# Moving the first expert's input and a set of matrix copies into the attention of a two-layer transformer, and adding unread products at its start

## The chip, the cores and the metric

The kernel runs on one core of a Trainium2 chip. A core has a matrix engine (TensorE, PE in the profile), a vector engine (VectorE, DVE), a scalar engine (ScalarE, ACT), GpSimd (POOL) and SyncE (SP), which here does nothing but issue DMA transfers. Each engine works through its own queue in order, and waits on semaphores for others. The metric is the time of one launch in microseconds (us). A profile also lists the clock that TensorE was granted, as a share of its full speed.

## The reference, cut to what matters

The input is 2048 tokens (4 x 512 in layer 0) of width 256. Each layer takes the normalised input and adds an attention and a mixture of experts to it:

```
x  = L0_attn_x
xn = layernorm(x)
x  = x + attention0(xn) + experts0(xn)
xn = layernorm(x)
x  = x + attention1(xn) + experts1(xn)
```

- attention0: 16 heads of width 16 over 4 key/value heads, queries and keys through low-rank products (64 and 32), rotary positions, causal softmax, output product.
- experts0: 8 experts, the best 2 for every token. Each expert takes at most 1280 rows (256 wide) and computes `(gelu(rows @ Wa) * (rows @ Wg)) @ Wout`, with 512 columns in each half; the result times the gate is added to the token's row.
- attention1: attention of every token to 32 learned patterns with sparsemax in place of softmax.
- experts1: 8 small gated experts (width 128), the best 2 for every token, and two shared ones.

## The kernel before, in words

*Start-up.* Tokens are taken in groups of 512. For each group, `fetch` loads the rows into `xg` (two buffers), in two halves; the second half of group 0 is issued by ACT, all else by SP. VectorE takes the statistics (`bn_stats`), GpSimd the inverse roots by Newton steps, VectorE normalises, TensorE turns the rows by transposes (`flip`), and the low-rank products go to `low`, a tile of 104 partitions x 2048. Before these can be used in the scores, the key tiles `ks` are filled with a pattern of zeros and ones (`clean_k` on ACT, `clean_q` on GpSimd for the query tiles).

*Attention of layer 0.* It runs twice over the keys: once for the maxima (`s<-ks,q`, VectorE reductions, then `flip_max`, whose result `mtT` goes through `mr` into the query tiles by a DMA `q<-mr`), once for the scores (`sc<-q,ks`, exponentials `es` on ACT, masks on GpSimd, products `av`). A quarter of the tokens has its output projection (`po`) when its heads are done, and the sum `xo` is stored to `x1` in DRAM. The rows that go to the experts are scattered to `buf` in DRAM by GpSimd's indirect DMAs, 258 wide: 256 values, the row's place and its gate.

The order of all this is not left to the framework: a planner in the kernel keeps a model of each engine's time (`T`, with constants such as `ISSUE = 620` ns for one DMA issue), picks the next piece of TensorE work among `candidates()`, and emits pieces for other engines from a list of `jobs`. `later(engine, duration, ready, f, then, rank)` puts a piece on that list, due from `ready` (in ns of the model's time), and `flush` emits it when the model has the engine free. Each instruction that it emits is pinned in program order by `pin`, `mm`, `flip` and `sdma`. Instructions that are not pinned are placed by the framework's scheduler.

*Experts of layer 0.* For each of 8 experts: `load_rows` brings 1152 rows of `buf` into `rows` by one DMA, `transposed` turns them with 18 transposes into `inT`, `places` copies out the rows' places (`to`) and gates, and `feed_forward` works in three chunks of 384 rows: for four column blocks, `pa` and `pg` (four instructions each), Gelu on ACT, product `hT` on VectorE; then three products `py` over `hT`, scaled to `ys` on VectorE, and added to `x1` by GpSimd's indirect DMAs. Rows of expert e+1 are loaded during expert e, weights of expert e+2 after it. (More than 1152 rows of one expert are dealt with behind a condition that is not met here.)

*Layer 1.* Its first matrices (`wqT`, `wk`, `wv` and seven smaller ones) are loaded by ACT's queue at the end of the attention and folded in the experts' stage. Its experts read their matrices with indirect DMAs from `wall`, a DRAM tile that 40 copies from DRAM to DRAM fill: five for each expert, two of them of `fg`, two of `fu`, one of `fd`. In the source they stand in the loop over layer 0's experts; the scheduler put all 40 at the head of SP's queue. Layer 1 then follows a plan of its own.

The PSUM pools of the attention are `ps2`, `pssc` and `psav`; those of the experts' stage `moetp` and `moeps`.

Of the kernel before, what the change touches and what calls it, by code (L numbers as in the profile page):

```python
# [145 lines left out]
def moe_transformer_kernel(  # L146
# [122 lines left out]
    csp = cctx.enter_context(tc.tile_pool(name="csp", bufs=1, side="right"))  # L269
    cs_sb = csp.tile([P, 2, S], F32, name="cs_sb")  # L270

    wi0 = cs_sb[:, 0].rearrange("p (c f) -> p c f", c=2)
    wt0 = cs_sb[:, 1, 0:4 * E].rearrange("p (c e) -> p c e", c=4)
    with ExitStack() as actx:
# [9 lines left out]
        psav = actx.enter_context(tc.tile_pool(name="psav", bufs=1, space=PSUM))  # L284
        low = attw.tile([96 + NE, NT], F32, name="low")
        wq16 = attw.tile([64, 2, 16, 16], F32, name="wq16")
# [28 lines left out]
        def sdma(*args):  # L315
            pin(SP.dma_start(*args))
# [52 lines left out]
        def lows(grp):  # L369

            ps = ps2.tile([P, 512], F32, tag="ps2", name="lw")
            for dc in range(2):
                mm(ps[:96 + NE], lhsT=wa_sb[:, dc], rhs=st[grp]["xnT"][:, dc], start=dc == 0, stop=dc == 1)
            pin(A.copy(low[:, 512 * grp:512 * grp + 512], ps[:96 + NE]))

# [264 lines left out]
        def load_out_weights():  # L640
# [3 lines left out]
            sdma(bout_sb, bout.broadcast_to([P, E]))  # L644

        xss = {}
        ways = bass_types.dram_disjoint_views(buf[:], 4)
# [8 lines left out]
        def dispatch(ti, k):  # L656
# [3 lines left out]
                                     xss[ti], None, bounds_check=NSLOT - 1, oob_is_err=False))  # L660

# [431 lines left out]
        def candidates():  # L1093
# [59 lines left out]
        while pos["av"] < len(avq) or jobs or projects or scat["ti"] < NTILE:  # L1153
            prefetch()
            refetches()
            keys_back()
            scatter()
            flush()
            cand = [z for z in candidates() if z[1] < INF]

            events = [job[4] for job in jobs if job[4] > T["PE"]] + [T["S"], T["V"], T["G"], T["A"]]
            events = [t for t in events if t > T["PE"]]
            best = min(cand, key=lambda z: z[:2]) if cand else None
            if best and best[1] <= min(events + [INF]) + 400:
                best[2]()
# [48 lines left out]

    sq = {}
# [3 lines left out]
    kp_sb = fold_tile(P, 2, NPAT)  # L1219
    A.dma_start(kp_sb, kpT.rearrange("(c p) m -> p c m", p=P))  # L1220
    bqk = fold_tile(P, 2, 2)
    A.dma_start(bqk, bqk2)
    bv_sb = fold_tile(1, E)
    A.dma_start(bv_sb, bv)
    A.dma_start(wo_sb, wo.rearrange("(c p) m -> p c m", p=P))
    A.dma_start(bo_sb, bo.broadcast_to([P, E]))
    A.dma_start(gw_sb, gw.rearrange("(c p) m -> p c m", p=P))
    A.dma_start(lb_sb, lb)


    with tc.tile_pool(name="moe", bufs=2) as mp, tc.tile_pool(name="moeh", bufs=3) as hp, \
            tc.tile_pool(name="moetp", bufs=2, space=PSUM) as mtp, \
            tc.tile_pool(name="moeps", bufs=2, space=PSUM) as mps:
        tiles = CAP0 // P

        def load_rows(e):
            rows = mp.tile([P, tiles, ROW], F32, tag="rows", name="rows")
            SP.dma_start(rows, buf[CAP * e:CAP * e + CAP0].rearrange("(c p) d -> p c d", p=P))
            return rows
# [20 lines left out]
        def feed_forward(wi, wt, inT, n, to, gates_e, c0, x1s):  # L1260
# [22 lines left out]
        last = bass_types.dram_disjoint_views(x1[:], 3)  # L1283
        rows = load_rows(0)
        for e in range(NE):
            wi, wt = experts[e]
            to, gates_e = places(rows, tiles)
            inT = mp.tile([P, 2, CAP0], F32, tag="inT", name="inT")
            transposed(rows, tiles, inT)
            if e + 1 < NE:  # L1290
                rows = load_rows(e + 1)
            for c in range(2):
                SP.dma_start(wall[P * e:P * e + P, P * c:P * c + P], fg[:, c, e])
# [760 lines left out]
```

## Time and profile before

| what | value |
|---|---|
| median of 3 runs | 2124.32 us (2123.4 to 2124.34) |
| the profiled execution's own time | 2125.51 us |
| its span, from the first to the last instruction | 2123.8 us |
| mean granted clock of TensorE | 0.952 |
| start-up, to the first score tile | 0 to 63.0 us |
| attention of layer 0, to the last `po` | 63.0 to 1201.0 us |
| seam: to the first expert's transposes | 1201.0 to 1209.3 us |
| experts of layer 0 | 1209.3 to 1605 us |
| layer 1 | 1605 to 2124 us |

How to read the profile's rows. A row of the timeline has the start in us, the duration in us (of a group of several instructions, from the first to the last), the engine (`SPq` and `ACTq` are DMA issues by that engine, `PEld` a weight load), the source line, the operation, output and inputs by the program's names, shape and type, and the count. In brackets stands the idle time before the instruction, and whose work ended it. A row of the table by stretch has the stretch, its length, the busy time and count of instructions for PE, PEld, DVE, ACT and POOL, the granted clock, the DMA engines' busy share and the GB/s moved. On the page, `PEclk` has one digit for each of 40 equal slices of the span, in tenths of full speed (9 is 0.9 and more).

### The profile page before, as it was taken

How to read it: one execution, taken by the hardware profiler on the slowest of the kernel's cores; microseconds unless marked ns; L12 is line 12 of the kernel's file. 1: busy time of each engine (PE TensorE's matmuls, PEld its weight loads, DVE VectorE, ACT ScalarE, POOL GpSimd, SP SyncE). 2: the span in 40 equal slices, each digit the busy share in tenths (PEclk: the TensorE clock that was granted, in tenths of full speed). 3: DMA queues.
4: the chain of work that ended last, by engine and by line, in shares of the span. 5: the costliest groups of instructions: out<-in, count | busy, mean ns of one | idle time of the engine just before them, and what ended most of it. 6: DMA issues, size and time to landing. Idle time of an engine off the chain costs nothing. (4 is left out here: it accounts for less than half of the span.)

```text
span 2123.8 us, 26286 instructions
## 1 busy us (share of the span) xinstructions
PE 1927.7 (91%) x9525; PEld 1070.7 (50%) x9534; DVE 1386.4 (65%) x1943; ACT 913.7 (43%) x1834; POOL 721.2 (34%) x914
## 2 busy tenths in 40 slices
PE   4689999899999999999999799999998998878886
PEld 2344443444444444444443366666765755666664
DVE  4576688676787578778784122222226599999896
ACT  3044456355555655665567411111112333554452
POOL 5232211443444333431101022222230088466551
PEclk8599899899999999999999899999999799999999
DMA  5433321242132322321200333333223022444417
GB/s 148 127 118 103 101 71 38 82 130 67 59 101 84 100 91 64 92 85 32 91 11 11 123 82 75 77 77 77 52 28 105 11 80 88 134 146 145 154 59 238
DMA packets 141384, 188.98 MB, mean 89 GB/s; under 512 B 15678, under 2 KB 109252, under 8 KB 141251
## 3 DMA queue, kind: packets, MB, share of 16 engines
q1 hardware_dynamic: 114672, 135.03, 21.1%
q0 software_dynamic: 23552, 50.46, 9.4%
q10 hardware_dynamic: 3026, 1.77, 0.3%
q8 instruction: 77, 1.26, 0.2%
q14 instruction: 57, 0.46, 0.1%
HBM read 100.74 MB, written 90.66 MB: 90 GB/s over the span
## 5 line engine op out<-in xcount | busy, mean ns | idle before, releaser
L510 ACT ACTIVATE es<-sc 128x512 f32<-128x512 f32 (+3 forms) x1280 | 599.6, 536 | 457.7 <-PE sc L310 447.0
L471 DVE TENSOR_REDUCE part<-s 128x2 f32<-128x1024 f32 (+3 forms) x640 | 650.4, 1059 | 210.5 <-PE s L310 209.3
L310 PE MATMUL sc<-q,ks 128*128 128x512 f32 (+3 forms) x1280 | 425.5, 418 | 19.5 <-ACT es L510 18.9
L310 PEld LDWEIGHTS sc<-q,ks 128*128 128x128 f32 x1280 | 211.7, 191 | 249.0 <-ACT es L510 174.5
L310 PE MATMUL av<-es,va 128*32 128x512 f32 (+3 forms) x2560 | 303.2, 552 | 3.4 <-POOL es L512 1.8
L512 POOL TENSOR_SCALAR_AFFINE_SELECT es<-es 128x256 f32<-128x256 f32 x256 | 103.4, 407 | 561.5 <-ACT es L510 560.5
L310 PE MATMUL s<-ks,q 64*128 64x512 f32 (+3 forms) x1280 | 253.1, 447 | 33.8 <-DVE part L471 11.2
L138 DVE TENSOR_TENSOR srt<-srt 128x1024 f32<-128x1024 f32 (+3 forms) x224 | 224.0, 1036 | 7.6 <-ACT to L138 0.5
L310 PEld LDWEIGHTS s<-ks,q 64*128 64x128 f32 x1280 | 111.6, 189 | 200.6 <-DVE part L471 110.5
L1279 POOL DMA_INDIRECT x<-ys,to x72 | 111.5, 1549 | 294.6 <-DVE ys L1277 165.5
L1270 DVE TENSOR_TENSOR hT<-ge,pg 128x384 f32<-128x384 f32 x96 | 53.2, 554 | 178.1 <-PE pg L1267 176.9
L1269 ACT ACTIVATE ge<-pa 128x384 f32<-128x384 f32 x96 | 47.1, 490 | 269.4 <-PE pa L1267 269.4
L138 POOL DMA_INDIRECT oe<-xn,to x80 | 109.3, 1367 | 76.0 <-ACT xn L138 56.2
L1267 PE MATMUL pa<-inT,wi 128*128 128x384 f32 x336 | 123.3, 486 | 0.0
L1267 PE MATMUL pg<-inT,wi 128*128 128x384 f32 x336 | 122.1, 486 | 0.0
L138 POOL DMA_INDIRECT buf<-xn,slot x64 | 87.7, 1371 | 99.9 <-DVE rc L138 80.7
L1274 PE MATMUL py<-wt,hT 128*128 128x256 f32 x504 | 112.2, 379 | 0.0
L138 ACT COPY srt<-srt 128x1024 f32<-128x1024 f32 (+2 forms) x80 | 67.2, 840 | 101.6 <-DVE srt L138 89.4
L310 PEld LDWEIGHTS av<-es,va 128*32 128x32 f32 x2560 | 55.7, 109 | 100.5 <-issue 76.3
L1274 PEld LDWEIGHTS py<-wt,hT 128*128 128x128 f32 x504 | 95.8, 190 | 17.5
L1277 DVE TENSOR_SCALAR ys<-py,gates 128x256 f32<-128x256 f32 x72 | 34.8, 484 | 86.0 <-PE py L1274 86.0
L1267 PEld LDWEIGHTS pg<-inT,wi 128*128 128x128 f32 x336 | 63.3, 190 | 42.7
(265 smaller groups left out, 2308.2 us busy)
## 6 DMA issues: line engine op xcount, KB each, us to landing
q<-qd SPq DMA_DIRECT2D x64, 256.0 KB
buf<-zero SPq DMA_DIRECT2D x20, 516.0 KB
buf<-zero SPq DMA_DIRECT2D x20, 514.0 KB
xn<-buf SPq DMA_DIRECT2D x20, 514.0 KB
rows<-buf SPq DMA_DIRECT2D x8, 1161.0 KB
qd<-hi SPq DMA_DIRECT2D x16, 512.0 KB
qd<-lo SPq DMA_DIRECT2D x16, 512.0 KB
xn<-oe SPq DMA_DIRECT2D x16, 512.0 KB
```

The costliest lines, as they stand in the source:

```text
L138: return lambda *a, **k: self.tc.keep_in_program_order(f(*a, **k))
L310: pin(PE.matmul(*args, **kw))
L471: pin(V.tensor_reduce(parts[j][:, i, 2 * pair:2 * pair + 2, kb], sc[:, :, :n], AX.X, ALU.max))
L510: pin(A.activation(es[:, g % 2, :n], sc[:, :n], AF.Exp, scale=0.25))
L512: pin(G.affine_select(es[:, :, 0:P], es[:, :, 0:P], pattern=[[0, 2], [1, P]], compare_op=ALU.is_ge, fill=0.0, base=0, channel_multiplier=-1))
L1267: PE.matmul(ps[:, :n], lhsT=wi[:, dc, col:col + P], rhs=inT[:, dc], start=dc == 0, stop=dc == 1)
L1269: A.activation(ge[:, :n], pa[:, :n], AF.Gelu)
L1270: V.tensor_tensor(hT[:, f, :n], ge[:, :n], pg[:, :n], ALU.mult)
L1274: PE.matmul(py, lhsT=hT[:, f, P * i:P * i + P], rhs=wt[:, f], start=f == 0, stop=f == 3)
L1277: V.tensor_scalar(ys, py, gates_e[:, c:c + 1], None, ALU.mult)
L1279: G.indirect_dma_start(x1s[c % len(x1s)], bass.IndirectOffsetOnAxis(ap=to[:, c:c + 1], axis=0), ys, None, compute_op=ALU.add)
```

## The change

It has six parts.

1. The 40 copies into `wall` are now pinned in the attention by `copy_matrices`, in eight sets of five, due from 320 us of the model's time on, one set every 60 us.
2. `clean_k(0)` is no longer emitted ahead of everything: all five fills are jobs due from 2, 7, 12, 17 and 22 us. In the new order ACT issues the second half of group 0's load first.
3. Unread products: in model time in which TensorE has nothing to do, before the first `av`, a bf16 product of the tile of ones (128x256) is emitted for every 160 ns, into a `psav` tile that nobody reads. There are 98: 48 at the head of TensorE's queue, 2 and then 48 after the third group's transposes and low-rank products, before the first score tile.
4. The first expert's rows: three SP loads of 384 rows (`load_rows0`) after the last scatter, and 18 transposes with three VectorE copies (`turn_rows0`) after the last maxima. They lie in `low`, which now has all 128 partitions and outlives the attention, and in `cs_sb`. The experts' stage starts with these, so `load_rows(0)` and `transposed` for expert 0 go.
5. Ten loads for layer 1 go from ACT's queue to SP's, in the loop at e = 1 (`load_fold`).
6. `py` has a PSUM pool of its own, and the two buffers of `rows` are a part of `low` and one tile.

On TensorE the seam now has this order: the last `av`, one `po`, two `pa` of the first expert, seven `po`, then `pg` and `pa` of the first expert in turn.

```diff
-        low = attw.tile([96 + NE, NT], F32, name="low")
+    low = csp.tile([P, NT], F32, name="low")
+    rows0 = low[:, 0:CAP0 // P * ROW].rearrange("p (c d) -> p c d", d=ROW)
+    inT0 = [low[:, CAP0 // P * ROW + 768 * i:CAP0 // P * ROW + 768 * i + 768] for i in range(2)] + [cs_sb[:, 1, 4 * E:4 * E + 768]]
...
+        def copy_matrices(e):
+            for c in range(2):
+                sdma(wall[P * e:P * e + P, P * c:P * c + P], fg[:, c, e])
+                sdma(wall[P * e:P * e + P, E + P * c:E + P * c + P], fu[:, c, e])
+            sdma(wall[P * e:P * e + P, 2 * E:3 * E], fd[:, e])
...
+        def load_rows0(i):
+            sdma(rows0[:, 3 * i:3 * i + 3], buf[384 * i:384 * i + 384].rearrange("(c p) d -> p c d", p=P))
+        def turn_rows0(i):
+            tp = ps2.tile([P, 2, 512], F32, tag="ps2", name="tp0")
+            for dc in range(2):
+                for c in range(3):
+                    flip(tp[:, dc, P * c:P * c + P], rows0[:, 3 * i + c, P * dc:P * dc + P], ident)
+            pin(V.tensor_copy(inT0[i], tp[:, :, 0:384]))
...
+            if pos["u"] == len(units) and at.get("turned", 0) < 3:
+                i = at.get("turned", 0)
+                t = max(now, when("row0", i), free2[-2])
+                def turn():
+                    at["turned"] = i + 1
+                    t = use2(1500, "t", 0, lambda: turn_rows0(i))
+                    free2.append(on("V", 1000, t))
+                yield t - now + 200, t, turn
...
-        clean_k(0)
...
-        for i in range(1, NKS):
-            later("A", 2560, 6000 + 4000 * i, lambda i=i: clean_k(i), None, 2)
+        for i in range(NKS):
+            later("A", 2560, 2000 + 5000 * i, lambda i=i: clean_k(i), None, 2)
...
+        for e in range(NE):
+            later("S", 5 * ISSUE, 320000 + 60000 * e, lambda e=e: copy_matrices(e), None, 2)
...
+        idle = ones.bitcast(BF16)
+        def product():
+            if "idle" not in st[0]:
+                st[0]["idle"] = psav.tile([P, 512], F32, tag="av", name="idle")
+            mm(st[0]["idle"][:, 0:256], lhsT=idle[:, 0:P], rhs=idle, start=True, stop=True)
...
+                if pos["av"] == 0:
+                    idle_for += t1 - T["PE"]
+                    while idle_for > 160:
+                        idle_for -= 160
+                        if (not free2[-1] and idles < 48) or (when("low", 1) < INF and not pos["u"]):
+                            idles += 1
+                            product()
                 T["PE"] = t1
...
+            if at.get("w0") and scat["ti"] == NTILE and not at.get("r0"):
+                at["r0"] = 1
+                for i in range(3):
+                    later("S", ISSUE, T["PE"] + 8000, lambda i=i: load_rows0(i),
+                          lambda t, i=i: at.update({("row0", i): t}), 2)
...
-    for nm, ap in (("wqT", wqT), ("wk", wk), ("wv", wv)):
-        sq[nm] = fold_tile(P, 2, E)
-        A.dma_start(sq[nm], ap.rearrange("(c p) m -> p c m", p=P))
...
+    def load_fold():
+        for v, ap in ((sq["wqT"], wqT), (sq["wk"], wk), (sq["wv"], wv), (kp_sb, kpT), (wo_sb, wo), (gw_sb, gw)):
+            SP.dma_start(v, ap.rearrange("(c p) m -> p c m", p=P))
+        SP.dma_start(bqk, bqk2)
...
+            tc.tile_pool(name="moepy", bufs=2, space=PSUM) as mpy, \
...
+        rows_of = [rows0, mp.tile([P, tiles, ROW], F32, tag="rows", bufs=1, name="rows")]
         def load_rows(e):
-            rows = mp.tile([P, tiles, ROW], F32, tag="rows", name="rows")
+            rows = rows_of[e % 2]
...
-                py = mps.tile([P, E], F32, tag="py", name="py")
+                py = mpy.tile([P, E], F32, tag="py", name="py")
...
-        rows = load_rows(0)
+        rows = rows0
         for e in range(NE):
             wi, wt = experts[e]
             to, gates_e = places(rows, tiles)
-            inT = mp.tile([P, 2, CAP0], F32, tag="inT", name="inT")
-            transposed(rows, tiles, inT)
+            if e == 0:
+                parts_in = inT0
+            else:
+                inT = mp.tile([P, 2, CAP0], F32, tag="inT", name="inT")
+                transposed(rows, tiles, inT)
+                parts_in = [inT[:, :, s0:s0 + STEP] for s0 in range(0, CAP0, STEP)]
             if e + 1 < NE:
                 rows = load_rows(e + 1)
-            for c in range(2):
-                SP.dma_start(wall[P * e:P * e + P, P * c:P * c + P], fg[:, c, e])
-                SP.dma_start(wall[P * e:P * e + P, E + P * c:E + P * c + P], fu[:, c, e])
-            SP.dma_start(wall[P * e:P * e + P, 2 * E:3 * E], fd[:, e])
+            if e == 1:
+                load_fold()
             for s0 in range(0, CAP0, STEP):
-                feed_forward(wi, wt, inT[:, :, s0:s0 + STEP], STEP, to, gates_e, s0 // P, last if e == NE - 1 else [x1[:]])
+                feed_forward(wi, wt, parts_in[s0 // STEP], STEP, to, gates_e, s0 // P, last if e == NE - 1 else [x1[:]])
```

More of the change, by code (lines that the diff above doesn't have):

```diff
@@ L270, in moe_transformer_kernel @@
     cs_sb = csp.tile([P, 2, S], F32, name="cs_sb")
+    low = csp.tile([P, NT], F32, name="low")
+    rows0 = low[:, 0:CAP0 // P * ROW].rearrange("p (c d) -> p c d", d=ROW)
+    inT0 = [low[:, CAP0 // P * ROW + 768 * i:CAP0 // P * ROW + 768 * i + 768] for i in range(2)] + [cs_sb[:, 1, 4 * E:4 * E + 768]]
+    inT0 = [v.rearrange("p (c n) -> p c n", c=2) for v in inT0]
     wi0 = cs_sb[:, 0].rearrange("p (c f) -> p c f", c=2)
@@ L373, in lows @@
                 mm(ps[:96 + NE], lhsT=wa_sb[:, dc], rhs=st[grp]["xnT"][:, dc], start=dc == 0, stop=dc == 1)
-            pin(A.copy(low[:, 512 * grp:512 * grp + 512], ps[:96 + NE]))
+            pin(A.copy(low[:96 + NE, 512 * grp:512 * grp + 512], ps[:96 + NE]))
         def logits(grp):
@@ L1152, in moe_transformer_kernel @@
             later("S", ISSUE, 340000 + 40000 * i, lambda i=i: clear(buf1, i), None, 2)
-        while pos["av"] < len(avq) or jobs or projects or scat["ti"] < NTILE:
+        idle = ones.bitcast(BF16)
[3 more added lines that the diff above has]
+            mm(st[0]["idle"][:, 0:256], lhsT=idle[:, 0:P], rhs=idle, start=True, stop=True)
+        idle_for, idles = 0, 0
+        while pos["av"] < len(avq) or jobs or projects or scat["ti"] < NTILE or at.get("turned", 0) < 3:
             prefetch()
@@ L1213, in fold_tile @@
         return v
-    sq = {}
-    for nm, ap in (("wqT", wqT), ("wk", wk), ("wv", wv)):
-        sq[nm] = fold_tile(P, 2, E)
-        A.dma_start(sq[nm], ap.rearrange("(c p) m -> p c m", p=P))
[L1219 to L1228, printed above, removed]
+    sq = {nm: fold_tile(P, 2, E) for nm in ("wqT", "wk", "wv")}
+    kp_sb, bqk, bv_sb = fold_tile(P, 2, NPAT), fold_tile(P, 2, 2), fold_tile(1, E)
+    def load_fold():
+        for v, ap in ((sq["wqT"], wqT), (sq["wk"], wk), (sq["wv"], wv), (kp_sb, kpT), (wo_sb, wo), (gw_sb, gw)):
+            SP.dma_start(v, ap.rearrange("(c p) m -> p c m", p=P))
+        SP.dma_start(bqk, bqk2)
+        SP.dma_start(bv_sb, bv)
+        SP.dma_start(bo_sb, bo.broadcast_to([P, E]))
+        SP.dma_start(lb_sb, lb)
     with tc.tile_pool(name="moe", bufs=2) as mp, tc.tile_pool(name="moeh", bufs=3) as hp, \
             tc.tile_pool(name="moetp", bufs=2, space=PSUM) as mtp, \
+            tc.tile_pool(name="moepy", bufs=2, space=PSUM) as mpy, \
             tc.tile_pool(name="moeps", bufs=2, space=PSUM) as mps:
         tiles = CAP0 // P
+        rows_of = [rows0, mp.tile([P, tiles, ROW], F32, tag="rows", bufs=1, name="rows")]
         def load_rows(e):
-            rows = mp.tile([P, tiles, ROW], F32, tag="rows", name="rows")
+            rows = rows_of[e % 2]
             SP.dma_start(rows, buf[CAP * e:CAP * e + CAP0].rearrange("(c p) d -> p c d", p=P))
```

## The prediction

> **What bounds the kernel now.** I read the page first: busy totals, then the 40 slices of the granted clock. The page's chain of waits ended in layer 1, whose instruction order is the same in both kernels, so it says nothing of the stages that change.
>
> ```profile
> PE 1927.7 (91%) x9525; PEld 1070.7 (50%) x9534; DVE 1386.4 (65%) x1943; ACT 913.7 (43%) x1834; POOL 721.2 (34%) x914
> PEclk8599899899999999999999899999999799999999
> ```
>
> TensorE is busy for 91% of the span. The weak slices of the clock row are the second (53 to 106 us) and the one at the end of the attention (around 1200 us). So I took the timeline of the two seams, and the busy times by stretch. First the seam between attention and layer-0 experts:
>
> ```profile
> 1195.27 0.71 DVE L541 STREAM_TRANSPOSE att<-t3c 128x512 f32<-128x512 f32 x1 [0.74 <-POOL t3c L537]
> 1196.04 4.98 PE L310 MATMUL po<-wout_sb,att 128*128 128x256 f32 x14 [2.03 <-DVE att L541]
> 1201.04 0.36 SPq L1238 DMA_DIRECT2D rows<-buf  x1
> 1209.30 1.94 PE L1254 MATMUL tp<-ident,rows 128*128 128x128 f32 x8 [8.29 <-DMA rows<-buf]
> 1216.80 1.80 PE L1267 MATMUL pg<-inT,cs_sb 128*128 128x384 f32 x4
> 1218.44 1.45 PE L1267 MATMUL pa<-inT,cs_sb 128*128 128x384 f32 x4
> ```
>
> After the last output projection (`po`) TensorE stands 8.29 us for the first expert's rows, then turns them at half speed; the steady pace (one `pa` of 4 instructions in 1.45 us) begins at 1218.44. Now the stretches: length, busy time of PE, PEld, DVE, ACT, POOL, then granted clock, DMA share, GB/s.
>
> ```profile
> 54.00:58.00 4.00, 0.03 (x1) 0.00 (x0) 3.41 (x16) 0.58 (x1) 0.72 (x4) 0.87 0.43 126
> 63.00:80.00 17.00, 13.49 (x36) 5.44 (x36) 6.13 (x11) 1.01 (x1) 2.29 (x11) 0.50 0.40 111
> 80.00:104.00 24.00, 17.91 (x72) 10.12 (x71) 15.37 (x29) 2.42 (x4) 4.93 (x4) 0.50 0.38 112
> 125.00:129.00 4.00, 2.57 (x22) 1.29 (x24) 3.84 (x11) 1.76 (x5) 1.37 (x4) 0.95 1.08 281
> 1140.00:1190.00 50.00, 46.17 (x259) 17.43 (x262) 6.60 (x11) 38.88 (x81) 7.82 (x14) 1.00 0.04 12
> ```
>
> From 54 us TensorE is idle until the first score tile at 63.03; from there to 104 us it runs at half clock though it works three quarters of the time. In the last 50 us of the attention it is 92% busy and VectorE nearly free. Last, the start-up:
>
> ```profile
> 5.30 0.59 SPq L1293 DMA_DIRECT2D wall<-in_fg_dram  x1
> 11.52 0.38 ACTq L358 DMA_DIRECT2D xg<-in_x_dram  x1
> 11.94 5.00 ACT L336 ACTIVATE ks<-ones,onecol 128x512 fp32r<-128x512 f32 x8 [5.71 <-DMA wall<-in_fu_dram]
> 11.99 1.80 POOL L331 MEMSET q<- 128x2048 f32 x1
> 14.84 0.43 DVE L207 BATCH_NORM_STATS2 st<-xg 128x6 f32<-128x256 f32 x1 [6.39 <-DMA xg<-in_x_dram]
> 17.62 0.20 POOL L224 TENSOR_TENSOR sd<-rstd_sb 128x4 f32<-128x4 f32 x1 [3.83 <-DVE rstd_sb L217]
> 63.03 0.44 PE L310 MATMUL s<-ks,q 64*128 64x128 f32 x1 [9.00 <-POOL sd L225]
> ```
>
> The second half of the first token group (`xg`) is loaded from ACT's queue only at 11.52, because ACT stood behind a `wall` copy; VectorE waits 6.39 us for it, and GpSimd 3.83 us for VectorE.
>
> **The change part by part.** The sum is made against the profiled execution, 2125.5 us (span 2123.8), which stands 1.2 above the median of the runs, 2124.3. About 0.2%, 4 us, is what a measurement of this kernel can tell from no change.
>
> *Start-up.* In the changed order ACT issues the load of `xg` before its table load and its first `ks` fill, and no `wall` copy stands ahead of it. The load then lands about 9 us earlier and VectorE's statistics follow. GpSimd's Newton steps, which started at 17.62, are then held by GpSimd's own memset, which ends at 11.99 + 1.80 = 13.79. So 17.62 - 13.79 = **3.8 us** is gained. It carries through, since everything to 63.03 hangs in one line: norm, flips, freeing of the `xg` buffer, next load. Bounds: 1.5 (if a later load on the SP queue ends last) to 6 (if the queue, free of 24 us of issue, lets more than this come early). Taken: -3.8.
>
> *The copies of layer 1's matrices.* 40 SP issues of 0.60 us, 24 us, go from the head of the SP queue into the attention as 8 sets of 5, from about 320 us on, some 60 us apart. In the attention SP mostly waits: between 100 and 1193 us its largest wait, 360 us, is for VectorE's `mr`. A set costs 5 x 0.60 = 3.0 us of SP's time. Queued behind it are loads of `q` and `ks` for the scores; the last `q<-mr` was issued at 1147.62 and its scores begin at 1153.9, about 5 us after the issue ended (1148.96), so a set fits. The 3.1 MB run in stretches of light DMA traffic. Taken: 0; bounds 0 to +4.
>
> *Unread products.* 98 bf16 products 128x256, none of them read. From the nearest row, a 128x128 bf16 product at 0.61/4 us at half clock and 0.40/4 at full (at 64.72 and 1118.55), scaled to 256 columns and with its weight load, about 0.26 and 0.154 us each. The first 48 stand at the head of TensorE's queue and end near 13 us; TensorE then waits until about 19 us for the first flips and is cold again: nothing gained or lost. The other 50 follow the third group's flips, with 7 to 10 us of work in a gap of 9 us (54.03 to 63.03): hidden, and TensorE is warm at the first score tile. Does that last? Here the trace and the Trainium skill ("TensorE: Matmul & The Clock Gate", section "Why this matters for your kernels") part. The page has the clock fall only after TensorE idles for more than some 3 us at a stretch. In 63 to 104 no idle gap reached 1.5 us, so by that rule a warm start holds: 31.4 us of half-speed work (13.49 + 17.91) becomes 15.7, and up to some 14 us is gained before other engines bind. But in 125 to 129 TensorE was busy 2.57 of 4.00 us with no such gap, and the next stretch ran at 0.50. By the trace, a busy share of about two thirds over some 3.4 us drops the clock; at full speed the scores after 59 us would be about half busy, so it drops within one such window. Taken: -1; bounds +1 and -12.
>
> *Rows of the first expert, in the attention.* Three SP loads replace one, late in the attention, ahead of the last `q<-mr`: 3 x 0.6 us on SP, inside the 5 us of slack just named. 18 flips move into a stage where TensorE is 92% busy. The trace has them at 0.13 us (1.04 us for 8 at 1311) to 0.165 (0.66 for 4 at 51.43): 2.3 to 3.0 us. The same page (section "Part 4: PE-mode transpose") gives about 0.275 us for a bf16 one, which by an estimate would make 5.0 us; the trace has durations for this very shape, so they decide. Part may fall into the 8% that is idle. Taken: **+2.5**; bounds +1 and +4. The three VectorE copies of 128x768 that take the result hide in VectorE's 43 idle us of those 50. One set stands right before the last flip of maxima, so it and the `q<-mr` behind it come about 1 us later, again within the slack.
>
> *The seam.* Now TensorE's order after the last `av` is: `po` x1, two `pa` (which depend on a VectorE copy long done), seven `po`, then `pg` and `pa` of the first expert. The start of the seven is bound as before by `att` at 1196.0. The two `pa` fill the 2.03 us in which TensorE waited, so the clock should stay up: fourteen instructions at the full-clock pace of 0.43 us (the 256-wide products of layer 1 keep it) make 14 x 0.215 = 3.0 us instead of 4.98, end 1199.1. The first `pg` takes 1.3, and the `pa` of the second column block, the one that began at 1218.44, begins near 1200.4. Gain 1218.44 - 1200.4 = **18.0**. It is the 8.3 us of waiting, the flips and the half-clock `po`. Bounds: 13 (clock down over the whole seam: `po` 5 us, first products at half pace) to 18.5. Taken: -18.0.
>
> *What is late next.* On VectorE, which works in order, the first chunk now has, between its products `hT`, a cast `to<-rows` of expert 1 and one of expert 2, each waiting for a load, and later an `xn<-xn` waiting for layer 1's small matrices, whose 10 loads went from ACT's queue (4.8 us of issue) to the SP queue behind three weight loads. Behind each wait stand `hT`, and TensorE waits for `hT`'s `pg` buffers (two) and for `py`. Rows of expert 1 are issued near 1199; such a load took 8.3 us with traffic beside it and 6.8 in the middle of the experts (issued 1315.20, used 1321.99), so it is there by 1206 to 1207.5. VectorE reaches the cast near 1204.5. `py` begins no earlier than 1200.4 + 3 x 2.9 = 1209, so `hT` has room. Rows of expert 2 come about 4 us later (1.16 MB at the 269 GB/s of that stretch), near 1211, when the first `ys` is due. Taken: **+0.5**; bounds 0 and +4. GpSimd's order is unchanged in the whole kernel; layer 1's is on every engine, but for the queue of one load.
>
> Sum: -3.8 - 1 + 0 + 2.5 - 18.0 + 0.5 = -19.8. Profiled execution: 2105.7. Median: 2104.5.
>
> **The rivals.**
>
> *The clock holds through 63 to 104 us.* For: the page's rule, and TensorE is more than 75% busy there at half clock. Against: the row of 125 to 129. It adds another 11 or 12 us: about 2092.5.
>
> *The wait only moves.* The DMA queues ran at 269 to 352 GB/s at 1201 to 1218, and the changed kernel asks for rows of two experts, two experts' weights and ten matrices in the same 15 us. If VectorE stands for rows 2 or the small matrices until near 1220, and TensorE cools, 7 to 12 us of the 18 are given back: 2112 to 2116.
>
> *The unread products are themselves late.* If the clock is not up when the 50 begin, they take 50 x 0.26 = 13 us in a gap of 9, and the first score tile is 4 us late: the start-up gain is gone, 2108 to 2109.
>
> *Slower: SP's queue.* The sets of copies run on the queue that loads `q` and `ks` and returns `mr`. If a copy waits for a lane held by a slow transfer, the set is not 3.0 us but 3.0 plus that wait. A set that holds SP for T us costs TensorE T - 5. To eat 19.8 us, each of 8 sets has to hold SP for 7.5 us; at 8.2 us the loss is 26 and the time 2130. Against it: in the start-up the 40 copies went out every 0.64 us without a wait, and in the attention TensorE waited for `q<-qd` only 1.1 us in all.
>
> *It does not do what it says.* Loads, flips and copies do stand where the change says; only the unread products can fail: no clock gained, 2105.5.
>
> **How the numbers follow.** The sum as it stands, with each unknown within its near bounds (2098 to 2111): 0.60. Clock held, 2088 to 2097: 0.11. Wait moved, 2111 to 2118: 0.16. Late products, near 2109: 0.08. Slower: 0.05. The range 2095 to 2114 holds nearly all of the first and fourth, half of the third and a little of the second: about 0.8. Faster: all but the last case, 0.95; of its 0.05, 0.01 falls within 0.2% and 0.04 beyond.
>
> **What would show it.** In the profile after: BATCH_NORM_STATS2 of the second half near 8 us and the first score tile near 59; clock 1.0 at 59 and 0.50 again by about 64; 18 flips in the last 50 us of the attention at 0.13 to 0.17 us; no TensorE idle over 1 us from the last `po` to the first `pa`; the first expert's end at about 1311 - 20 = 1291; layer 1 as long as before, 519 us. It is wrong if the scores from 59 to 100 run at full clock, if a gap of more than 3 us waits for `rows` or `xn` after the seam, or if the waits for `q` and `ks` in the attention exceed a few us.

## The result, and the profile after

The changed kernel takes 2100.64 us at the median (2099.11 to 2102.17) against 2124.33 beside it; the ratio is 0.9883 (95% interval 0.987 to 0.9895). That is 23.7 us less. The prediction was 2104.5, with a range of 2095 to 2114. The profiled execution took 2102.17 us, with a span of 2100.4. One kernel's runs lie some microseconds apart here, because half-clock stretches of TensorE come at other places from run to run; so a step's size is read below from the start of one and the same instruction in two profiles, and small differences of medians are not trusted.

The page after:

```profile
PE 1933.4 (92%) x9632; PEld 1079.4 (51%) x9632; DVE 1386.8 (66%) x1943; ACT 912.7 (43%) x1831; POOL 714.0 (34%) x914
PEclk7699899899999999999999999999998799999999
```

The clock row's 23rd digit, the slice of the seam, was 8 and is 9; the dip that is left late in the row (8 and 7) is the start of layer 1. The timeline of the seam:

```profile
1186.20 0.72 DVE L536 STREAM_TRANSPOSE t<-av 128x512 f32<-128x512 f32 x1 [37.64 <-PE av L313]
1186.98 1.56 PE L1318 MATMUL pa<-low,cs_sb 128*128 128x384 f32 x4 [0.29 <-DVE t L536]
1188.71 3.29 PE L313 MATMUL po<-wout_sb,att 128*128 128x256 f32 x14 [0.18 <-DVE att L544]
1191.84 1.46 PE L1318 MATMUL pg<-low,cs_sb 128*128 128x384 f32 x4
1193.13 1.45 PE L1318 MATMUL pa<-low,cs_sb 128*128 128x384 f32 x4
1195.99 0.56 DVE L1321 TENSOR_TENSOR hT<-ge,pg 128x384 f32<-128x384 f32 x1 [1.54 <-PE pg L1318]
1198.53 0.17 DVE L1294 CAST to<-rows 128x9 int32<-128x9 f32 x1 [1.98 <-DMA rows<-buf]
1203.21 0.17 DVE L1294 CAST to<-low 128x9 int32<-128x9 f32 x1 [1.50 <-DMA low<-buf]
```

The two early `pa` fill the gap at the output projection, the fourteen `po` run at full clock, and the `pa` of the second column block starts at 1193.13, 4.42 us after the `po`; before it was 1218.44 - 1196.04 = 22.40. VectorE did meet the new waits for rows of experts 1 and 2, 1.98 and 1.50 us long, and they cost nothing: from 1186 to 1240 us TensorE has no gap above 0.3 us. By stretch (columns as before: length, PE, PEld, DVE, ACT, POOL, clock, DMA share, GB/s):

```profile
58.50:75.50 17.00, 13.42 (x36) 5.31 (x36) 6.21 (x11) 1.01 (x1) 2.79 (x13) 0.52 0.36 101
1132.00:1182.00 50.00, 47.23 (x270) 18.82 (x270) 9.38 (x14) 38.64 (x80) 7.58 (x14) 1.00 0.04 12
1192.00:1200.00 8.00, 8.00 (x27) 4.65 (x26) 2.75 (x8) 2.96 (x5) 0.40 (x2) 1.00 0.86 260
```

TensorE has no idle time in the 8 us after the seam. Scores from 58.5 us still run at half clock (the 0.52 of the first row is 0.6 us at full clock and then half). The start-up, and the three sets of transposes in the attention:

```profile
2.32 0.46 ACTq L361 DMA_DIRECT2D xg<-in_x_dram  x1
14.11 0.20 POOL L224 TENSOR_TENSOR sd<-rstd_sb 128x4 f32<-128x4 f32 x1
48.88 5.40 PE L313 MATMUL idle<-ones 128*128 128x256 bf16 x48
58.51 0.29 PE L313 MATMUL s<-ks,q 64*128 64x128 f32 x1 [4.22 <-POOL rstd_sb L227]
1137.58 0.82 PE L316 MATMUL tp<-ident,low 128*128 128x128 f32 x6
1142.51 0.82 PE L316 MATMUL tp<-ident,low 128*128 128x128 f32 x6
1144.78 0.84 PE L316 MATMUL tp<-ident,low 128*128 128x128 f32 x6
```

So the ledger of the two profiled executions reads: first score tile 63.03 to 58.51, 4.5 us earlier; the last `t<-av` (VectorE's copy of the last products with the values) 1193.53 to 1186.20, 7.3 earlier; second `hT` of the experts 1221.29 to 1195.99, 25.3 earlier, which makes 18.0 for the seam; end of the span 23.4 earlier. From the second `hT` to the last it is 378.7 us in both: the experts kept what they were given. What the attention added, 2.8 us, and layer 1 lost, 1.9 us, is looked at first.

The 18.0 us do not scatter. From the start of the last `t<-av` to that of the second `hT` it is 27.8, 27.8 and 27.6 us in the kernel before and its two variants below, and 9.8 us in all eight profiles of builds that have the changed kernel's seam.

### The profile page after: what moved, and what is told of

Its sections match the earlier page's. It is cut to its first block, busy times and chain, and to the rows that moved or that the text cites. A ratio compares the mean times of both kernels' runs of the same rounds, so it can differ in the third digit from the quotient of the medians.

```text
span 2100.4 us, 26488 instructions
## 1 busy us (share of the span) xinstructions
PE 1933.4 (92%) x9632; PEld 1079.4 (51%) x9632; DVE 1386.8 (66%) x1943; ACT 912.7 (43%) x1831; POOL 714.0 (34%) x914
## 3 DMA queue, kind: packets, MB, share of 16 engines
q1 hardware_dynamic: 116770, 136.26, 21.7%
## 5 line engine op out<-in xcount | busy, mean ns | idle before, releaser
L138 POOL DMA_INDIRECT buf<-xn,slot x64 | 81.2, 1268 | 101.0 <-DVE rc L138 81.8
L1325 PEld LDWEIGHTS py<-wt,hT 128*128 128x128 f32 x504 | 95.8, 190 | 17.5
```

Source lines behind the costliest of these rows:

```text
L138: return lambda *a, **k: self.tc.keep_in_program_order(f(*a, **k))
L1325: PE.matmul(py, lhsT=hT[:, f, P * i:P * i + P], rhs=wt[:, f], start=f == 0, stop=f == 3)
```

## The experiments

### What scatters: the changed kernel once more

> The changed kernel itself once more, for a second profile. Theory 1: part of the attention's change (two half-clock stretches of 3.4 us fewer near 930 us, two more near 395 us, against the kernel before) is a matter of where the clock's 3.4 us windows happen to fall in a run, and no work of the change; then this profile has its half-clock stretches elsewhere, and the time scatters by 2 to 3 us around 2100.6. Theory 2: the change itself moved them; then the stretches lie where they lay in the first profile, within a microsecond, and the attention is again 2.8 us shorter than in the kernel before.

Measured: 2101.67 us at the median (2101.2 to 2107.69). By stretch, first the first profile of the changed kernel, then the second:

```profile
214.00:244.00 30.00, 29.54 (x143) 13.29 (x142) 18.38 (x27) 13.00 (x28) 9.75 (x15) 0.77 0.29 82
905.00:940.00 35.00, 34.06 (x202) 15.25 (x202) 26.17 (x32) 20.68 (x43) 16.30 (x24) 1.00 0.42 120
```

```profile
214.00:244.00 30.00, 29.68 (x166) 13.45 (x164) 21.70 (x30) 15.71 (x34) 9.47 (x15) 0.89 0.39 110
905.00:940.00 35.00, 34.18 (x183) 15.38 (x184) 24.61 (x31) 18.72 (x40) 17.26 (x25) 0.90 0.44 125
```

The same instructions, TensorE as busy as before, and the clock was 0.77 and 1.00 in one run, 0.89 and 0.90 in the other. In the kernel before, the same part of the attention (910 to 945 us there) had 0.90. So the half-clock stretches wander, as theory 1 has it; one run of the four was 7 us above the others, more than it allowed. This repeat alone does not settle the 2.8 us, for its attention was again that much shorter, as theory 2 has it: from the first score tile to the last `t<-av` 1127.8 us, after 1127.7 in the first profile and 1130.5 in the kernel before. The other profiles below settle it. The kernel before and its two variants have the attention's instructions in one and the same order and took 1130.5, 1127.4 and 1123.0 us for it. The changed kernel and its builds with fewer unread products, again with one order among them, took 1127.2 to 1135.9. So 2.8 us is less than the scatter and is not credited to the change. It is the same with layer 1: from the last `ys` to the end of the last computing instruction it is 513.8 us in the kernel before, but 515.9 and 516.2 in its two variants, whose layer 1 is untouched, and 516.5 and 515.8 in the two profiles of the changed kernel. From the same instruction to its twin the two profiles drift apart by up to 3.7 us (between 276 and 366 us) and end 1.0 us apart.

### The start-up: the copies, or ACT's order?

The kernel before with the copies moved alone:

```diff
+        for e in range(NE):
+            later("S", 5 * ISSUE, 320000 + 60000 * e, lambda e=e: copy_matrices(e), None, 2)
...
-            for c in range(2):
-                SP.dma_start(wall[P * e:P * e + P, P * c:P * c + P], fg[:, c, e])
...
```

> The kernel before, with the 40 copies into wall moved into the attention and nothing else (the first ks fill still stands ahead of the second xg load on ACT). Theory 1: it is the copies at the head of the queues that cost the start-up; the xg load then goes out at about 6.3 us instead of 11.5, GpSimd's memset is again what the Newton steps wait for, and the later xg load (issued at 26.5 before, behind 33 copies) comes at about 23: first score tile 3.5 to 4.6 us earlier, 58.5 to 59.5, time 2120 to 2121. Theory 2: it is the order of ACT's first instructions: less than 1.5 us. The copies in the attention cost nothing: start of the last score stage moved by the start-up's gain and by the clock's scatter alone.

The kernel before with the first `ks` fill put off alone:

```diff
-        clean_k(0)
...
-        for i in range(1, NKS):
-            later("A", 2560, 6000 + 4000 * i, lambda i=i: clean_k(i), None, 2)
+        for i in range(NKS):
+            later("A", 2560, 2000 + 5000 * i, lambda i=i: clean_k(i), None, 2)
```

> The kernel before, with the first ks fill no longer first (all five fills are due later), and the 40 copies left at the head of SP's queue. Theory 1 (copies): the xg load of ACT goes out at 2.3 us, Newton starts at about 14, but the next xg load still stands behind 33 copies and goes out at 26.5 as before: the first score tile gains at most 1 us, 62 to 63, time 2123 to 2125. Theory 2 (order on ACT, which the prediction's 3.8 us rests on): 59 to 60, time 2120 to 2121.

Measured: the copies alone, 2118.55 us against 2123.43 beside it (ratio 0.9975, 0.9963 to 0.9987); ACT's order alone, 2125.13 (ratio 1.0006, 0.9996 to 1.0015). The first score tile of the one and then of the other:

```profile
58.06 0.44 PE L310 MATMUL s<-ks,q 64*128 64x128 f32 x1 [9.56 <-POOL sd L226]
```

```profile
13.48 0.20 POOL L224 TENSOR_TENSOR sd<-rstd_sb 128x4 f32<-128x4 f32 x1
25.36 1.02 SPq L358 DMA_DIRECT2D xg<-in_x_dram  x2
63.47 0.44 PE L310 MATMUL s<-ks,q 64*128 64x128 f32 x1 [9.50 <-DMA q<-qd]
```

With ACT's order alone the Newton steps started at 13.48 instead of 17.62, as the prediction wanted, and the first score tile did not move (63.47 against 63.03). The next `xg` load goes out at 25.36, behind the copies; it was at 26.50 in the kernel before, which is 5.3 us plus 33 copies at 0.64. That load also waits for the transposes that free its buffer. In the kernel before, the two end almost together, the transposes at 25.78 and the last copy ahead of it at 26.37:

```profile
24.66 1.12 PE L313 MATMUL tp<-ident,xg 128*128 128x128 f32 x4 [0.68 <-ACT xnT L367]
25.77 0.60 SPq L1293 DMA_DIRECT2D wall<-in_fg_dram  x1
26.50 1.01 SPq L358 DMA_DIRECT2D xg<-in_x_dram  x2
```

With the copies moved, and ACT's order as before:

```profile
3.68 0.38 ACTq L358 DMA_DIRECT2D xg<-in_x_dram  x1
20.73 1.12 PE L313 MATMUL tp<-ident,xg 128*128 128x128 f32 x4 [0.68 <-ACT xnT L367]
21.88 0.88 SPq L358 DMA_DIRECT2D xg<-in_x_dram  x2
```

Moving the copies ends both waits. ACT's own load goes out at 3.68 instead of 11.52, so that the transposes end at 21.85, and SP's queue is free for the load that follows them. The load is 4.6 us earlier, the score tile 5.0. So the copies give the start-up's gain, and ACT's new order adds nothing to it. A clear queue with ACT's load still late was not run; an estimate from these times, 26.37 - 25.78, gives it 0.6 us. In the attention the copies did no harm: between 300 and 780 us, where the changed kernel has all of them, TensorE waits for `q` loads

```profile
PE s L313 <- DMA q<-qd: 0.7, 2, 0.5
```

(total, times, longest), and 0.5 us in the same part of the kernel before.

### The unread products

Without any:

```diff
-                            product()
+                            pass
```

> The changed kernel without its 98 unread products. My theory: they are worth nothing beyond a microsecond, since the clock was back at half 0.6 us after the first score tile: 2100 to 2102, first score tile at 58.5 with 0.44 us instead of 0.29. Rival: they gain by a warm start, or keep the clock up later: 2104 or more. Other rival: they get in the way of TensorE's work: 2098 or less.

> The changed kernel without the 98 unread products, a second time, because the first (2106.3 at the median of 4 runs, but only 0.95 us later in the profile once the start-up is over) left open whether they are worth 1 or 5 us. Theory 1: 0.95 us by the warmer start, the rest was where the clock's windows fell: 2100.5 to 2103.5 at the median. Theory 2: they gain 3 to 5 us by keeping half-clock stretches away later: 2104.5 or more.

Without the first 48:

```diff
-                        if (not free2[-1] and idles < 48) or (when("low", 1) < INF and not pos["u"]):
+                        if when("low", 1) < INF and not pos["u"]:
```

> The changed kernel without the first 48 unread products (at the head of TensorE's queue), the other 50 kept. Theory 1: the first 48 are worth nothing, since TensorE is cold again at 11 us and first works at 19: 2100 to 2103, start-up as in the changed kernel within 0.3 us. Theory 2: it is they that make the difference: 2104.5 or more.

Measured: without any, 2106.32 (2101.34 to 2106.95) the first time and 2101.24 (2101.03 to 2101.65) the second; without the first 48, 2103.78 (2102.06 to 2109.55). The first of these fell on the rival's side and misled: its runs sit at 2101 and at 2106 to 2107, as one run in four of the unchanged repeat did (2107.69). All eight runs without products have a median of 2101.5, the eight of the changed kernel 2101.3. The second build bears out its theory 1. The third lies between its two theories; its profile has the first score tile at 58.16, none the later for it, and lost its time in the attention (1135.9 us), where the order of instructions is the changed kernel's. The products are worth nothing that these runs can show. In the profile of the second build the scores are within 0.1 us of the changed kernel's at 74 us, with the first tile at 58.46.

Then five more products after each piece of TensorE's work up to 100 us:

```diff
                 best[2]()
+                if pos["av"] == 0 and pos["u"]:
+                    for _ in range(5):
+                        product()
```

> The changed kernel with five more unread products after every piece of TensorE's work from the first score tile to the first product with the values (about 58 to 100 us), some 130 more. It tests what sets the clock there. If the busy share sets it, as the prediction took from the trace: five products are 0.56 us at full speed, TensorE is then busy nearly all the time, the clock stays at full from 59 us, and the stretch is shorter by up to 10 us: 2091 to 2098. If the clock falls all the same, each five take 1.07 us at half speed, of which a part is in TensorE's gaps: 5 to 20 us more, 2105 to 2120. If the stretch is bound by the hand-over between TensorE and VectorE and not by TensorE's pace, the clock goes up and the time does not change: 2099 to 2103.

Measured: 2113.2 us (2110.98 to 2115.62), 12.6 us slower at the median and 11.1 in the profile, nearly all of it lost by 140 us. By stretch:

```profile
62.00:70.00 8.00, 8.00 (x27) 3.62 (x27) 1.99 (x5) 1.01 (x1) 0.39 (x2) 0.50 0.37 114
70.00:80.00 10.00, 9.84 (x35) 4.10 (x33) 5.81 (x7) 0.62 (x1) 1.97 (x2) 0.50 0.01 2
```

TensorE was busy all the time and the clock stayed at half. So the busy share, by which the prediction argued, is not what the clock follows. Layer 1 of the changed kernel shows the same without any addition:

```profile
1626.00:1635.00 9.00, 9.00 (x43) 9.00 (x44) 4.04 (x23) 5.85 (x12) 0.00 (x0) 0.50 0.00 0
1628.92 1.95 PE L138 MATMUL tp<-ident,xn 128*128 128x128 f32 x8
1630.66 3.42 PE L138 MATMUL po<-gw_sb,xT 128*128 128x8 f32 x16
```

These are products with 8 columns between transposes; the weight loads, too, take all of the 9.00 us. Busy, in the profile, does not tell how much of the array's rows and columns is at work; in these stretches products with few rows (16 or 64) or few columns (8) take much of the time. That this is what counts is a guess that fits, and was not tested by itself.

### The seam, taken apart

Rows loaded in the attention, but turned at the seam:

```diff
-            if pos["u"] == len(units) and at.get("turned", 0) < 3:
+            if False:
...
-            if e == 0:
-                parts_in = inT0
-            else:
+            if True:
                 inT = mp.tile([P, 2, CAP0], F32, tag="inT", name="inT")
```

> The changed kernel with the first expert's rows loaded in the attention, but turned at the seam, as the kernel before did it (18 transposes with copies by ACT and VectorE, no pa between the output projections). It splits the seam's 18 us into the wait for rows and the turning. My reckoning: the wait was 8.3 us, the turning to the second column block 9.1 us at half clock, which is about 5.5 at full clock without the wait; so about 5 us slower than the changed kernel, 2104 to 2108. Rival: the 2 us gap at the output projection lets the clock fall and the turning costs the full 9 us again: 2109 to 2112. Other rival: transposes in the attention cost as much as they save here: 2100 to 2102.

Rows loaded and turned at the seam (the same, and):

```diff
-        rows_of = [rows0, mp.tile([P, tiles, ROW], F32, tag="rows", bufs=1, name="rows")]
+        rows_of = [mp.tile([P, tiles, ROW], F32, tag="rows", bufs=1, name="rows"), rows0]
...
-        rows = rows0
+        rows = load_rows(0)
```

Here the three early loads are left out as well:

```diff
-            if at.get("w0") and scat["ti"] == NTILE and not at.get("r0"):
+            if False:
```

> The changed kernel with the whole old seam: the first expert's rows are loaded after the attention by one transfer and turned there. Mine: the seam's 17.9 us come back, less the 0.8 us that the transposes cost in the attention: 2117 to 2120, and TensorE waits 7 to 8 us for rows. Rival: with layer 1's loads behind the rows on SP's queue the rows arrive sooner, and some 3 us of the wait are not the seam's but those loads': 2112 to 2116.

Layer 1's ten loads on ACT's queue again:

```diff
-            SP.dma_start(v, ap.rearrange("(c p) m -> p c m", p=P))
+            A.dma_start(v, ap.rearrange("(c p) m -> p c m", p=P))
...
+    load_fold()
...
-            if e == 1:
-                load_fold()
```

> The changed kernel with the ten loads for layer 1 back on ACT's queue. My theory: their queue is worth nothing, the stretch after the last output projection keeps its pace: 2099.5 to 2102. Rival: on SP they come after the rows of experts 1 and 2 and leave those the DMA engines; back on ACT, rows come later and VectorE waits for them: 2 to 5 us more, 2103 to 2106.

Measured at the median: 2117.1 (2108.35 to 2133.25), 2118.15 (2114.34 to 2134.06) and 2117.38 (2109.61 to 2136.01). All three scatter far more than the changed kernel, with a mean clock between 0.957 and 0.939, and why is not known; so again the timelines decide. The rows-early kernel, then the one with the old seam:

```profile
1196.10 4.98 PE L313 MATMUL po<-wout_sb,att 128*128 128x256 f32 x14 [2.02 <-DVE att L544]
1207.09 1.45 PE L1318 MATMUL pa<-inT,cs_sb 128*128 128x384 f32 x4
```

```profile
1188.00 4.98 PE L313 MATMUL po<-wout_sb,att 128*128 128x256 f32 x14 [2.02 <-DVE att L544]
1193.01 0.37 SPq L1289 DMA_DIRECT2D rows<-buf  x1
1199.74 3.42 PE L1305 MATMUL tp<-ident,rows 128*128 128x128 f32 x16 [6.77 <-DMA rows<-buf]
1205.81 1.45 PE L1318 MATMUL pa<-inT,cs_sb 128*128 128x384 f32 x4
```

From the start of those fourteen `po` to the `pa` of the second column block it is 22.40 us in the kernel before, 17.81 with the old seam in the changed kernel, 10.99 with the rows early, 4.42 in the changed kernel. So turning in the attention, with the gap at the output projection filled, is worth 6.6 us (1.7 of it the `po` at full clock), the rows' early load 6.8, and 4.6 belong to what else differs between the kernel before and the old seam. There three of layer 1's ten loads go out on SP's queue beside the rows; in the kernel before, eight had gone out on ACT's by the time the rows were used. The rows land after 6.73 us instead of 8.26, and the turning runs at a clock that came back sooner. The separate PSUM pool of `py` is in these 4.6 us too and was not tested by itself; and the old seam has one profile only. For the turning the 5 us expected were 6.6, since after the 2 us gap most of `po` ran at half clock (4.98 us in all). For the old seam the median lies where I had it, but the seam itself speaks for the rival: 13.4 us (17.81 - 4.42), not 17.9.

The fourteen `po` show what filling the gap does. In the five profiles in which TensorE waits 2.0 us ahead of them (the kernel before, its two variants and these two) the clock falls within 1 us after the gap and they take 4.98 us. In the nine in which the `pa` fill it they take 3.29.

The medians of all three lie above what the seam explains, by 10, 4 and 7 us. Their lowest runs do not: 2108.35, 2114.34 and 2109.61, where the changed kernel's median with 6.6, 13.4 and, for the third, 9.4 us (below) makes 2107.2, 2114.0 and 2110.0.

With the ten loads on ACT's queue the second `pa` still starts 4.42 us after the `po`, but then, in the waits of 1186 to 1215 us (total, times, longest):

```profile
ACT L1322 <- DMA gw_sb<-in_gw_dram: 17.5, 1, 17.5
DVE to L1296 <- DMA rows<-buf: 7.3, 1, 7.3
PE tp L1307 <- DMA rows<-buf: 5.0, 1, 5.0
```

ACT stands in its own queue of loads: 17.5 us from its last exponential to the Gelu's table load, 7.0 in the changed kernel, and the first `ge` is some 10 us later. The framework's scheduler also puts expert 1's transposes ahead of the third column block, where they wait 5 us for rows, and the clock falls. From there the kernel is 9.4 us later (0.9 before the seam, 10.3 after). That is a third of what its profiled run lost, which is 27 us; some 17 more go in layer 1, most of them after 2050 us, with a clock of 0.68 in the last 67 us (0.93 in the last 50 of the changed kernel), and that loss is not explained. My expectation of no effect was wrong, and the rival's 2 to 5 us too small. The delay of ACT and the changed order were not separated.

### A version that goes further

The nine loads of the output matrix are not needed for hundreds of microseconds, and stand in SP's queue ahead of the `q` of the first score tile; in the changed kernel:

```profile
48.06 5.10 SPq L319 DMA_DIRECT2D wout_sb<-in_wout_dram  x8
53.84 2.57 SPq L319 DMA_DIRECT2D q<-qd  x4
```

```diff
-        later("S", 9 * ISSUE, 40000, load_out_weights, None, 2)
+        later("S", 9 * ISSUE, 100000, load_out_weights, None, 2)
```

> The changed kernel with the nine loads of the output matrix and its bias (first used by po, hundreds of us later) due at 100 us of the model's time instead of 40. In the changed kernel they hold SP's queue from 48.1 to 53.8 us, ahead of the loads of q that the first score tile waits for; the planner then also emits 18 of the last 48 unread products. If SP's queue bounds the first score tile: it begins at 52.5 to 54 instead of 58.5, time 2095 to 2098. If something else is late next (rows of the next groups on GpSimd and VectorE): 56 to 58, time 2098 to 2101.

And with GpSimd's fourth and fifth fill later:

```diff
-            later("G", 2000, 3000 * i, lambda i=i: clean_q(i), None, 2)
+            later("G", 2000, 30000 + 3000 * i, lambda i=i: clean_q(i), None, 2)
```

> The same, and GpSimd's fourth fill of a q tile (1.8 us at 12.2 us, ahead of the first Newton steps, VectorE's next steps stretched beside it) due 30 us later. If the Newton steps bound the start: Newton begins at 12.5 instead of 14.1, first score tile another 1 to 1.6 us earlier, 2093.5 to 2097. If not: as the kernel beside it.

Measured: 2102.75 us (2097.46 to 2106.5) and 2101.29 (2095.01 to 2103.24). The first score tiles of the two:

```profile
53.42 0.29 PE L313 MATMUL s<-ks,q 64*128 64x128 f32 x1
```

```profile
52.10 0.32 PE L313 MATMUL s<-ks,q 64*128 64x128 f32 x1
```

The start is 5.1 and 6.4 us earlier, as expected, and the time is not shown to be better than the changed kernel's: the lowest run of the second is 4 us below the changed kernel's lowest, the medians are no lower. Against the changed kernel's profile the first of the two is 8.0 us earlier when the experts begin, 7.3 after the first expert and 4.7 at the end; the mean clock of these runs is 0.946 to 0.952, against 0.954 to 0.958 in the changed kernel. The planner also orders the attention differently after the earlier start. The two profiles have that order in common and took 1124.8 and 1133.0 us for the attention, so whether it costs anything cannot be told from scatter. Around the first kernel's first score tile there was also this:

```profile
50.00:54.30 4.30, 2.57 (x8) 0.89 (x6) 2.06 (x10) 0.90 (x1) 1.18 (x6) 1.00 0.73 186
54.30:57.00 2.70, 2.33 (x14) 1.68 (x15) 0.76 (x2) 0.11 (x1) 1.90 (x10) 0.50 1.05 294
```

The clock fell at 54.3 us, with no wait of TensorE longer than 1.1 us in the 4 us before.

## Why the prediction was right, and where not

*Seam, -18.0.* Right in size: 18.0. Right in mechanism for the wait and the turning, and the two `pa` kept the clock up: `po` took 3.29 us, 3.0 were reckoned. Incomplete in what belongs to it. I booked the ten loads' move to SP's queue only as a danger (+0.5, bounds 0 to +4). The runs show it as a part that the seam needs: on ACT's queue they keep ACT idle for 17.5 us instead of 7.0, and that build is 9.4 us slower there.

*What is late next, +0.5.* 0: the waits were where they were expected, 1.98 and 1.50 us for rows on VectorE, and TensorE stayed full.

*Start-up, -3.8.* The gain is 4.5. The line of work that the step follows is there: Newton steps 3.5 us earlier (14.11 for 17.62), the `xg` load after them 4.2 earlier (22.31 for 26.50). What was wrong is that this line alone sets the end, and that ACT's order frees it. ACT's order by itself gave nothing: the buffer then came free at 21.62, and SP's queue, 33 copies long, held the load until 25.36. And the copies' move frees ACT's load without the new order. The queue stood in the sum only as a bound. The size came out near because one part of the change happens to end both waits; that is luck as far as the stated cause goes.

*Unread products, -1.* 0. Their mis-sized term was the duration: 48 took 5.40 us, 0.11 each, not 0.154, so they ended 4.2 us ahead of the score tile they were to warm. The first tile did run at full clock (0.29 us for 0.44), and 0.6 us later the clock was at half. That it would not hold was right; the reason, a busy share under two thirds, fell with the filled stretch. The rule of the Trainium skill that was weighed against it ("TensorE: Matmul & The Clock Gate", "Why this matters for your kernels": the clock drops after an idle gap above some 3 us) agrees with the 4.2 us gap here. The section does not say that such a gap is the only cause, as the prediction read it, and here it is not: the clock also fell after the 2.0 us gap before `po`, and at 54.3 us in the kernel with the later loads, where no gap was above 1.1.

*Transposes in the attention, +2.5.* +0.8, from the shift of `t<-av` across them: by the times of the kernel before, it is 8.2 us earlier at 1156 and 7.3 at 1194. It does not scatter: the last two `t<-av` start 38.6 us apart in all nine profiles with these transposes and 37.8 in the five without (the interval ahead of it is 0.15 us shorter with them). Six take 0.82 us, 0.14 each with overlap, and two thirds fell into TensorE's idle time, which I allowed for only in the bound. The 0.275 us that the prediction weighed and set aside is of the size of one transpose's own duration, 0.27 us here; in a row they start 0.11 us apart, so durations must not be added.

*Copies in the attention, 0.* Confirmed.

The sum of the steps as measured is -4.5 + 0 + 0 + 0.8 - 18.0 + 0 = -21.7, predicted -19.8; the remaining 2 of the 23.7 lie within what the clock scatters. The errors partly cancel: the products gave 1 us less than was put down, the other steps together 2.9 more. None of the rivals came true: the clock did not hold, the wait did not move, the products were not late, SP's queue carried the copies. One of the signs named the wrong expert: 1311 us is the end of the second one's last product (1311.45), which moved to 1286.18; the first one's moved from 1262.52 to 1237.25.

## What to carry to other kernels

Between an early wait and the end of a stage, check each queue for what stands in it: an engine can be relieved of a wait for a load without any gain, when the next load sits behind 33 copies in another queue that ends half a microsecond later. A stage's first input is best loaded and turned inside the stage before, and what issues transfers there must not be the engine that the new stage needs first. Microseconds of a median mean little while the clock's half-speed stretches wander; compare one instruction's start in two profiles, and profile the same kernel twice before explaining a part of it.

## What the runs showed of the hardware that was not expected

- TensorE can be busy for 8.00 of 8.00 us and stay at a granted clock of 0.50, with unread products of 128x256 between products of 16 and 64 rows; in layer 1 it is 9.00 of 9.00 with 8-column products and transposes. It can lose the clock after a gap of 2.0 us, in five profiles of five, and without a gap above 1.1 us.
- Transposes of 128x128 in 32-bit floats last 0.27 us each and start 0.11 us apart at full clock: six in 0.82 us.
- The same instructions in two runs of one kernel had clocks of 0.77 and 0.89 (214 to 244 us) and of 1.00 and 0.90 (905 to 940 us); runs of one kernel fell at about 2101 and about 2107 us.
- ACT, issuing ten loads in a row while others fill the DMA engines, was held from 1192.92 to 1203.00 us and stood 17.5 us between its last work and its next, against 7.0 without them; one issue itself is about 0.5 us.
